# Storing x1's first channel with a graph's inputs, and later queue places for the gates' weights, spectra, loads and sixth product

## The chip, the core and the metric

The kernel runs on one core of one Trainium2 chip. The core has a matmul engine (TensorE, with its weight loads shown apart), a vector engine (VectorE, DVE in profiles), an activation engine (ScalarE, ACT), a general engine (GpSimd, POOL), a sync engine (SyncE, SP) that here only issues DMAs, and 16 DMA engines that all queues share. Each engine works through its own queue in order; a semaphore wait at the head of a queue holds everything behind it. The metric is the time of one execution on the device in microseconds (us).

## What is computed

64 graphs of N = 256 nodes with D = 256 features go through two layers. `adj` is each graph's matrix.

```python
# layer 0
norm_adj = deg**-0.5 * adj * deg**-0.5            # deg = row sums
x1 = layernorm(x + ((norm_adj + alpha*I) @ x) @ W.T + b)
# layer 1: three branches of x1
h      = relu(bn1(conv1(x1)))                     # a 1x1 convolution
x_conv = relu(bn2(conv2(h)) + x1)                 # 17 taps along the nodes
s      = x1 @ w_se.T + b_se
A      = exp(-dist(s))                            # squared distances of all pairs
x_nmp  = A @ relu(x1 @ w_msg.T + b_msg)
# a GRU cell joins them
gi = concat(x_conv, x_nmp) @ w_ih.T + b_ih
gh = x1 @ w_hh.T + b_hh
out = layernorm(x1 + gru(gi, gh, x1))
```

All numbers are 32-bit floats.

## The kernel before, in words

**Stages.** The graphs form four quarters of Q = 16. For each graph `layer0` (L383) makes x1, normalises it and stores it to DRAM as `x1_d` (L461, ACT's queue). `layer1` (L474) transposes x1 into `xn` (L464), multiplies by the conv1 weights (L487) and the message weights (L508), transforms h along the nodes into spectra in the big tile `VM`, and makes x_nmp. `graphs` (L1083) weaves layer 1 of one graph with layer 0 of the graph two further on.

When a quarter's 16 graphs are in `VM`, conv2 is done there as products of spectra (`products`, L611) with the transformed conv2 weights, which stream in from DRAM through six `u` buffers (`load_u`, L579, SP's queue), and then the inverse transform on VectorE, whose results go to DRAM as `xc_d` (L782).

Last come the gates of the quarter's graphs, `gru` (L914). Its product of 256x768 inputs with the weights is done by seven smaller products of halves (p1 to p7), which need four sums of halves of the inputs (`input_sums`, L893, POOL) and combined weights in `wall`. Each of the seven is three matmul calls, line L930.

**What overlaps.** Quarter 0's first 16 graphs run alone with the setup: in 13 parts (`weights`, L316) the conv2 weights are loaded (`load_taps`), multiplied on TensorE, summed on VectorE and POOL (L339, L340) and written to DRAM as `ud` by POOL's DMAs (L342). Then the gates' weights are prepared (`gate_weights`, L1156): a first piece loads them (L1160 to L1174), a second mends them on VectorE, further pieces subtract them from one another (L1189). The list `others` (L1193) says which of these pieces goes with which graph. Later, a quarter's first four gates (`EARLY`) run between the next quarter's last graphs, and the other twelve between its spectral products and inverse transform. The last quarter's 16 gates end the kernel, from about 1797 us on.

**The inputs of the gates.** `xn` has four blocks of 128 channels by 256 nodes: x1's first half with its first channel replaced by the constant 1 (so that the biases ride on that row, L471), two blocks of x_nmp, and x1's second half. It is stored whole as `xn_d` (L568) and read back into the tile `inputs` by `load_gate` (L838). Two more blocks of `inputs` receive the convolution, plus x1, through ReLU. For 28 of the graphs (`in_blocks`, L820: the first four of each quarter, and all of the last) `transposed` (L864) does this with VectorE's block transpose, and then POOL adds the x1 blocks (L875). That adds 1 in place of channel 0, so `load_gate` also loads channel 0 of x1 into a row of its own (L844), POOL adds it (L876), and the ReLU's bias is `less_one`, the bias less 1 in that row. The other 36 graphs add x1 in a DMA and transpose on TensorE.

**What sets the order.** The program is traced piece by piece; a scheduler at build time then gives each engine its order. It prefers what was traced earlier, but fills an engine that would be idle with later work that it believes ready. `tc.issue_after(i)` holds an instruction back: it keeps whatever is traced inside it, on i's engine, behind i in that engine's queue; it adds no wait. DMAs that SP and ACT issue share eight semaphores in turn, so such a DMA can also wait for an earlier one, of any kind, that used the same semaphore.

Of the kernel before, what the change touches and what calls it, by code (L numbers as in the profile page):

```python
# [9 lines left out]
F32 = mybir.dt.float32  # L10
AF = mybir.ActivationFunctionType
ALU = mybir.AluOpType
AX = mybir.AxisListType

P = 128
# [5 lines left out]
def bcast_rows(v, n, rows=P):  # L21

    return bass.AP(tensor=v.tensor, offset=v.offset, ap=[[0, rows], [1, n]])
# [3 lines left out]
def kernel(  # L27
# [38 lines left out]
    RB = 32  # L66
# [40 lines left out]

    def load_x(g):
        xin[g] = loads.tile([P, NCH, D], F32, name="x_t")
        nc.sync.dma_start(xin[g], x[g].rearrange("(c p) f -> p c f", p=P))  # L110

    def load(g):
        if g < B:
# [55 lines left out]
    bn_t = const.tile([P, D], F32)  # L169

    bn2_bias = const.tile([P, DCH], F32)
    less_one = const.tile([P, DCH], F32)

    def batch_norms(pool):

# [197 lines left out]
    xn_d = [dram.tile([P, 2 * DCH, N], F32, name=f"xn_d{g}") for g in range(B)]  # L373
    XN = {}
    ALONE = set()
    EXP, WEIGHED, NORMED = {}, {}, []
    gate = None
    EAGER = {0, Q - 4, Q - 3, Q - 2, *range(Q, Q + 13), 2 * Q + 5, 2 * Q + 6, 3 * Q + 5, 3 * Q + 6}
# [95 lines left out]
    def layer1(g, place):  # L474
# [9 lines left out]
        for c in range(NCH):  # L484
            p = bank("p_conv1")[:, : D + NSE]
            for k in range(DCH):
                nc.tensor.matmul(  # L487
                    p, x1T[:, k, c * P : (c + 1) * P], wc1[:, k, :], start=k == 0, stop=k == DCH - 1
                )
            nc.scalar.activation(  # L490
                h[:, c].rearrange("p (k a) -> p k a", k=DCH), p[:, :D].rearrange("p (a k) -> p k a", k=DCH), AF.Relu
            )
            EVICTED[g] = nc.scalar.copy(cols[:, c, :, :NSE], p[:, D:].unsqueeze(1).to_broadcast([P, 4, NSE])).ins
# [71 lines left out]
                    start=mc == 0, stop=mc == NCH - 1,  # L565
                )
        AGGREGATED[g] = nc.scalar.copy(xn[:, 1 : 1 + DCH], p).ins
        nc.scalar.dma_start(xn_d[g], xn)  # L568
        yield


# [4 lines left out]

    TILES, AWAY = [V], []

    def load_u(n, i):  # L579
        u = ustream.tile([P, DCH, D], F32, name="u")  # L580
        nc.sync.dma_start(
            u, ud[i][n * GC : (n + 1) * GC].rearrange("c g o -> (c g) o")[:D].rearrange("(p k) o -> p k o", k=DCH)
        )
        return u

    def product(p, j, v, u, onto=False):
# [225 lines left out]
            yield from output(q, n + 12, im + 3, re + 3)  # L812


    GATE, CONV, SUMS, OWN, CHANNEL = {}, {}, {}, {}, {}


    EARLY = 4

    def in_blocks(g):  # L820
        return g % Q < EARLY or g >= B - Q

    def load_conv(g):
        y = xc_d[g // Q][g % Q]
        if in_blocks(g):


            CONV[g] = gate.tile([P, DCH, N // RB, RB], F32, name="xc_blocks", tag="xc_g")
            for b in range(NB):
                nc.sync.dma_start(  # L830
                    CONV[g][b * RB : (b + 1) * RB],
                    y.rearrange("(s r) (k b j) -> b r k s j", r=RB, k=DCH, j=RB)[b],
                )
            return
        CONV[g] = gate.tile([P, NCH, D], F32, name="xc_g")
        nc.sync.dma_start(CONV[g], y.rearrange("(c p) d -> p c d", p=P))

    def load_gate(g):  # L838
        inputs = GATE[g] = gate.tile([P, 3 * DCH, N], F32, name="inputs")
        nc.sync.dma_start(inputs[:, : 2 * DCH], xn_d[g])  # L840
        if in_blocks(g):
            CHANNEL[g] = gate.tile([1, N], F32, name="channel", bufs=1)
            with nc.allow_non_contiguous_dma("one channel"):
                nc.sync.dma_start(CHANNEL[g], x1_d[g // Q][g % Q][:, 0:1].rearrange("n d -> d n"))  # L844

    def load_x1(g):
        OWN[g] = gate.tile([P, NCH, D], F32, name="x1_g")
        nc.sync.dma_start(OWN[g], x1_d[g // Q][g % Q].rearrange("(c p) d -> p c d", p=P))

    def sent(g):  # L850

# [12 lines left out]
    def transposed(g):  # L864

        inputs = GATE[g]
        xcT = inputs[:, 2 * DCH :]
        if in_blocks(g):
            to = xcT.rearrange("p k (s r) -> p k s r", r=RB)
            if g < B - Q:  # L870
                with tc.issue_after(WEIGHED[max(WEIGHED)]):
                    nc.vector.transpose(to, CONV.pop(g))
            else:
                behind(nc.vector.transpose(to, CONV.pop(g)))
            nc.gpsimd.tensor_tensor(xcT, xcT, inputs[:, 0 : 2 * DCH : 2 * DCH - 1], op=ALU.add)  # L875
            JOINED.append(nc.gpsimd.tensor_tensor(xcT[0:1, 0], xcT[0:1, 0], CHANNEL.pop(g), op=ALU.add).ins)  # L876
            with tc.issue_after(EXP[max(EXP)]):
                for k in range(DCH):
                    nc.scalar.activation(xcT[:, k], xcT[:, k], AF.Relu, bias=less_one[:, k : k + 1])
            return  # L880
        xc = CONV.pop(g)
        p = bank("p_xcT").rearrange("p (k n) -> p k n", k=DCH)
        for k in range(DCH):
            for c in range(NCH):
                nc.tensor.transpose(p[:, k, c * P : (c + 1) * P], xc[:, c, k * P : (k + 1) * P], ident)
        for k in range(DCH):
            nc.scalar.activation(xcT[:, k], p[:, k], AF.Relu, bias=bn2_bias[:, k : k + 1])
# [26 lines left out]
    def gru(g):  # L914
# [10 lines left out]
        def product(a, b, p=None):  # L925
            first = p is None
            if first:
                p = accbank("p_g")
            for k in range(HALF):
                nc.tensor.matmul(  # L930
                    p[:, : 3 * HD] if k == 0 else p[:, HD:], a[:, k], wall[:, b, k].rearrange("p t d -> p (t d)"),
                    start=first and k == 0, stop=True, skip_group_check=not first or k > 0,
                )
            return p
# [8 lines left out]
        yield  # L943
        if following:
            sent(g + 1)
        p6 = product(S[2], T2)
        mark(nc.vector.tensor_add(quarter(0, 1), first, p6), 1)  # L947
        nc.vector.tensor_add(quarter(1, 1), quarter(0, 1), p7)  # L948
        product(A12, B21, p1)
# [84 lines left out]
    def chain(*stages):  # L1034
        for stage in stages:
            yield from stage

    def take(stage, n):

        for _ in range(n):  # L1040
            if next(stage, "end") == "end":
                return
            yield

    def later(stage):
        yield
        yield from stage
# [74 lines left out]
    with tc.tile_pool(name="setup", bufs=1) as setup:  # L1122
# [31 lines left out]
        nc.gpsimd.tensor_copy(wmsg[0:1, 0], biases[:, NSE:])  # L1154

        def gate_weights():  # L1156
            for b, i, h in ((B11, 0, 0), (T1, 0, 1), (B21, 1, 0), (B22, 1, 1)):
                at = slice(h * HD, (h + 1) * HD)
                own = w_hhT[i * P : (i + 1) * P].rearrange("p (t d) -> p t d", t=3)
                nc.sync.dma_start(wall[:, b, 0, 0:1], own[:, 2:3, at])  # L1160
                nc.sync.dma_start(wall[:, b, 0, 1:3], own[:, 0:2, at])
                for k in range(DCH):
                    row = (D if i == 0 else 0) + k * P
                    nc.sync.dma_start(
                        wall[:, b, 1 + k], w_ihT[row : row + P].rearrange("p (t d) -> p t d", t=3)[:, :, at]
                    )
            nc.gpsimd.tensor_copy(less_one, bn2_bias)
            nc.gpsimd.tensor_tensor(less_one[:, 0:1], less_one[:, 0:1], unit, op=ALU.subtract)
            top = setup.tile([P, 3, 2, HD], F32, name="hh_top", tag="taps", bufs=2)
            nc.sync.dma_start(top.rearrange("p t h d -> p (t h d)"), bcast_rows(w_hhT, 3 * D))  # L1170
            rows = setup.tile([1, 2, 3, 2, HD], F32, name="gate_bias", tag="taps", bufs=2)
            for i, v in enumerate((b_hh, b_ih)):
                nc.sync.dma_start(rows[:, i].rearrange("p t h d -> p (t h d)"), v.rearrange("(a d) -> a d", a=1))
            nc.sync.dma_start(bn_t, bcast_rows(b_ih[2 * D :], D))  # L1174
            yield

            for b, i, h in ((B11, 0, 0), (T1, 0, 1), (B21, 1, 0), (B22, 1, 1)):
                with tc.issue_after(marks[-1][0]):
                    w = wall[:, b, 0]
                    nc.vector.tensor_sub(w[:, GR : GZ + 1], w[:, GR : GZ + 1], top[:, 0:2, h])  # L1180
                    nc.vector.tensor_sub(w[:, GN], w[:, GN], top[:, 2, h])
                    if i == 0:
                        nc.vector.tensor_add(w[0:1, GR : GZ + 1], rows[:, 0, 0:2, h], rows[:, 1, 0:2, h])
                        nc.vector.tensor_copy(w[0:1, GN], rows[:, 0, 2, h])
            yield

            for to, a, b in ((T3, B22, T1), (T1, T1, B11), (T2, B22, T1), (T4, B21, T2)):
                with tc.issue_after(marks[-1][0]):
                    nc.vector.tensor_sub(wall[:, to], wall[:, a], wall[:, b])  # L1189
                yield  # L1190
# [1 line left out]
        more_weights = gate_weights()  # L1192
        others = [weights(setup, i, scale2) for i in range(NPARTS)]  # L1193
        others[0] = later(others[0])
        others += [take(more_weights, i) for i in (1, 3, 2)]
        run(graphs(0, range(Q), others))
    ustream = ctx.enter_context(tc.tile_pool(name="ustream", bufs=6))

# [156 lines left out]
```

## Time and profile before

| | us |
|---|---|
| three runs | 2043.63, 2042.55, 2040.06 |
| median | 2042.55 |
| profiled execution | 2048.04 |
| its span, first to last instruction | 2046.3 |
| TensorE busy | 1984.9 |
| VectorE busy | 1396.4 |
| ScalarE busy | 964.7 |
| POOL busy | 698.1 |

The profile comes from one execution with the profiler on, and its lines name the engine, the source line, the operation, what is written and read, the shape, and the count. In a timeline line, the first number is the start, the second the time taken, both in us from the span's start; a bracket tells how long the engine had been idle and what ended that. In the table of waits the numbers are the total, the count and the longest. A window line has the stretch, its length, the busy time of TensorE, its weight loads, VectorE, ScalarE and POOL with instruction counts, the granted TensorE clock (1.00 is full), the busy share of the DMA engines and the GB/s they moved. In the chain, a line has start, length and name of one step in a sequence in which each step was released by the one before it. A line "x28: a/b/c" has the shortest, median and longest duration in ns. A busy TensorE is modelled from pipelined matmuls.

### The profile page before, as it was taken

How to read it: one execution, taken by the hardware profiler on the slowest of the kernel's cores; microseconds unless marked ns; L12 is line 12 of the kernel's file. 1: busy time of each engine (PE TensorE's matmuls, PEld its weight loads, DVE VectorE, ACT ScalarE, POOL GpSimd, SP SyncE). 2: the span in 40 equal slices, each digit the busy share in tenths (PEclk: the TensorE clock that was granted, in tenths of full speed). 3: DMA queues.
4: the chain of work that ended last, by engine and by line, in shares of the span. 5: the costliest groups of instructions: out<-in, count | busy, mean ns of one | idle time of the engine just before them, and what ended most of it. 6: DMA issues, size and time to landing. Idle time of an engine off the chain costs nothing. (4 is left out here: it accounts for less than half of the span.)

```text
span 2046.3 us, 26391 instructions
## 1 busy us (share of the span) xinstructions
PE 1984.9 (97%) x8157; PEld 1437.7 (70%) x8157; DVE 1396.4 (68%) x3199; ACT 964.7 (47%) x2285; POOL 698.1 (34%) x679
## 2 busy tenths in 40 slices
PE   7999999999999999999999999999999999999997
PEld 6878788878667766777777766777777855555554
DVE  6334447787567788764546888874445899877787
ACT  5666654567442234566653233556664233333333
POOL 4444411232532143223322234322331045445543
PEclk8999999999999999999999999999999999999999
DMA  4766557544555654343336665334344745443431
GB/s 133 221 202 207 182 193 240 169 140 135 138 149 192 212 126 134 115 129 109 103 109 185 211 170 134 119 117 125 97 116 142 259 124 135 127 100 87 102 87 54
DMA packets 269021, 298.05 MB, mean 146 GB/s; under 512 B 84276, under 2 KB 211336, under 8 KB 268882
## 3 DMA queue, kind: packets, MB, share of 16 engines
q1 hardware_dynamic: 208842, 200.37, 33.8%
q10 hardware_dynamic: 44472, 67.39, 9.3%
q0 software_dynamic: 15568, 28.62, 6.3%
q8 instruction: 66, 1.08, 0.2%
q14 instruction: 73, 0.60, 0.1%
HBM read 193.19 MB, written 103.06 MB: 145 GB/s over the span
## 5 line engine op out<-in xcount | busy, mean ns | idle before, releaser
L930 PE MATMUL p_g<-wall,sums 128*128 128x384 f32 x1536 | 534.0, 488 | 6.1 <-POOL sums L901 3.2
L930 PEld LDWEIGHTS p_g<-wall,sums 128*128 128x128 f32 x1536 | 284.8, 190 | 193.4 <-issue 9.6
L930 PE MATMUL p_g<-wall,inputs 128*128 128x384 f32 x1152 | 406.8, 489 | 12.2 <-DVE G L948 12.2
L930 PEld LDWEIGHTS p_g<-wall,inputs 128*128 128x128 f32 x1152 | 215.3, 190 | 167.2 <-DVE G L948 27.8
L356 POOL TENSOR_TENSOR ln_rs<-ln_rs,neg_half 128x2 f32<-128x2 f32 x129 | 95.2, 738 | 546.7 <-DVE ln_rs L355 411.0
L901 POOL TENSOR_TENSOR sums<-inputs 128x384 f32<-128x384 f32 x128 | 143.1, 1118 | 329.0 <-PE p_g L930 303.2
L554 DVE TENSOR_TENSOR aT<-aT,adjT 128x512 f32<-128x512 f32 x64 | 45.2, 706 | 200.5 <-ACT aT L551 200.4
L435 POOL TENSOR_TENSOR x_t<-x_t,b_t 128x512 f32<-128x512 f32 x64 | 101.9, 1592 | 215.3 <-ACT x L432 138.8
L589 PE MATMUL p_k<-u,VM 128*128 128x256 f32 x736 | 169.6, 380 | 2.8 <-DMA u<-ud 1.6
L589 PEld LDWEIGHTS p_k<-u,VM 128*128 128x128 f32 x736 | 138.5, 190 | 25.6 <-PE p_k L589 2.5
L364 ACT ACTIVATE x_g<-x_g,ln_mr,ln_rs 128x256 f32<-128x256 f32 x128 | 70.0, 593 | 169.4 <-DVE ln_mr L360 164.6
L977 ACT ACTIVATE G<-G 128x512 f32<-128x512 f32 (+1 forms) x129 | 81.0, 628 | 128.7 <-DVE G L1004 91.9
L440 PE MATMUL p_hT<-adjT,x 128*128 128x256 f32 x512 | 125.7, 389 | 5.8 <-ACT x L432 2.3
L487 PE MATMUL p_conv<-wc,xn 128*128 128x259 f32 x512 | 126.5, 389 | 4.2 <-ACT xn L471 3.5
L563 PE MATMUL p_nmp<-aT,msg 128*128 128x256 f32 x512 | 121.4, 380 | 2.2 <-DVE aT L554 2.2
L450 PE MATMUL p_out<-w,hT 128*128 128x256 f32 x512 | 121.5, 380 | 0.9 <-ACT hT L445 0.7
L901 POOL TENSOR_TENSOR sums<-inputs,sums 128x384 f32<-128x384 f32 x64 | 74.8, 1169 | 138.0 <-PE p_g L930 137.9
L508 PE MATMUL p_msg<-wmsg,xn 128*128 128x256 f32 x512 | 121.9, 381 | 0.0
L487 PEld LDWEIGHTS p_conv<-wc,xn 128*128 128x128 f32 x512 | 99.1, 194 | 27.1 <-ACT xn L471 4.3
L526 PE MATMUL p_dft<-fwd,h 128*128 128x240 f32 x512 | 114.1, 366 | 0.0
L950 ACT COPY G<-p_g 128x512 f32<-128x512 f32 x64 | 37.4, 584 | 155.9 <-PE p_g L930 107.2
L450 PEld LDWEIGHTS p_out<-w,hT 128*128 128x128 f32 x512 | 95.6, 190 | 21.2 <-ACT hT L445 2.9
(173 smaller groups left out, 3596.9 us busy)
## 6 DMA issues: line engine op xcount, KB each, us to landing
u<-ud SPq DMA_DIRECT2D x284, 256.0 KB
xn_d<-xn ACTq DMA_DIRECT2D x64, 512.0 KB
inputs<-xn_d SPq DMA_DIRECT2D x64, 512.0 KB
ud<-u_set POOLq DMA_DIRECT2D x39, 480.0 KB, 6.3
adj_t<-in_adj_dram SPq DMA_DIRECT2D x64, 256.0 KB
x_t<-in_x_dram SPq DMA_DIRECT2D x64, 256.0 KB
x_d<-x ACTq DMA_DIRECT2D x64, 256.0 KB
xc_d<-VM SPq DMA_DIRECT2D x64, 256.0 KB
```

Of the source, the lines that this page charges most:

```text
L356: nc.gpsimd.tensor_tensor(rs[:, : len(chunks)], rs[:, : len(chunks)], neg_half[:, : len(chunks)], op=ALU.pow)
L435: nc.gpsimd.tensor_tensor(x_t, x_t, b0_t.unsqueeze(1).to_broadcast([P, NCH, D]), op=ALU.add)
L440: nc.tensor.matmul(p[:, k, :], x1[:, mc, k * P : (k + 1) * P], adjT[:, mc, 1 - mc : 3 - mc, :].rearrange("p n q -> p (n q)"), start=mc == ...
L450: nc.tensor.matmul(p[:, c, :], hT[:, k, c * P : (c + 1) * P], w0[:, k, :], start=k == 0, stop=k == DCH - 1)
L487: nc.tensor.matmul(p, x1T[:, k, c * P : (c + 1) * P], wc1[:, k, :], start=k == 0, stop=k == DCH - 1)
L508: nc.tensor.matmul(p[:, c, :], x1T[:, k, c * P : (c + 1) * P], wmsg[:, k, :], start=k == 0, stop=k == DCH - 1)
L526: nc.tensor.matmul(p[:, t0 * FL : t1 * FL], h[:, c, k * P : (k + 1) * P], fwd[:, first : first + t1 - t0, :].rearrange("p t f -> p (t f)") ...
L563: nc.tensor.matmul(p[:, k, :], msg[:, mc, k * P : (k + 1) * P], aT[:, mc].rearrange("p n q -> p (n q)"), start=mc == 0, stop=mc == NCH - 1,)
L589: nc.tensor.matmul(p[:, j * D : (j + 1) * D], v[:, k, :], u[:, k, :], start=k == 0 and j == 0 and not onto, stop=k == DCH - 1, skip_group_ ...
L901: nc.gpsimd.tensor_tensor(S[i], x, y, op=op)
L930: nc.tensor.matmul(p[:, : 3 * HD] if k == 0 else p[:, HD:], a[:, k], wall[:, b, k].rearrange("p t d -> p (t d)"), start=first and k == 0, ...
L977: nc.scalar.activation(rz, rz, AF.Tanh, scale=0.5)
```

## The change

1. For the 28 graphs `in_blocks`, the store of `xn` is split: blocks 1 to 3 by ACT as before, block 0 without its first row by SP, and its first row is copied from channel 0 of `x1_d` by SP. After POOL has added the x1 blocks, a memset puts the constant 1 back into that row of `inputs`. The load of the channel, its addition and `less_one` are gone.
2. `load_conv`, `load_gate` and `load_x1` are held, in SP's queue, behind the last u load that was traced before them (`behind_u`).
3. In the early gates, the sixth product is held behind the last conv1 matmul that was traced before it.
4. The first piece of `gate_weights` is held, in SP's queue, behind the last x load traced before it (graph 16's).
5. The third piece of the last `weights` part (the sum and the stores of the spectra) is traced late in graph 13 in place of the end of graph 12, and the loads of the gates' weights at the end of graph 13 in place of its beginning.

```diff
     def load_x(g):
         xin[g] = loads.tile([P, NCH, D], F32, name="x_t")
-        nc.sync.dma_start(xin[g], x[g].rearrange("(c p) f -> p c f", p=P))
+        xin["last"] = nc.sync.dma_start(xin[g], x[g].rearrange("(c p) f -> p c f", p=P)).ins
...
+    CONV1 = {}
+    EARLY = 4
+
+    def in_blocks(g):
+        return g % Q < EARLY or g >= B - Q
...
-                nc.tensor.matmul(
+                CONV1[g] = nc.tensor.matmul(
                     p, x1T[:, k, c * P : (c + 1) * P], wc1[:, k, :], start=k == 0, stop=k == DCH - 1
-                )
+                ).ins
...
-        nc.scalar.dma_start(xn_d[g], xn)
+        if in_blocks(g):
+            nc.scalar.dma_start(xn_d[g][:, 1:], xn[:, 1:])
+            nc.sync.dma_start(xn_d[g][1:, 0], xn[1:, 0])
+            with nc.allow_non_contiguous_dma("one channel"):
+                nc.sync.dma_start(xn_d[g][0:1, 0], x1_d[g // Q][g % Q][:, 0:1].rearrange("n d -> d n"))
+        else:
+            nc.scalar.dma_start(xn_d[g], xn)
...
+    LAST_U = {}
+
+    def behind_u():
+        return tc.issue_after(LAST_U[0])
+
     def load_u(n, i):
         u = ustream.tile([P, DCH, D], F32, name="u")
-        nc.sync.dma_start(
+        LAST_U[0] = nc.sync.dma_start(
...
     def load_gate(g):
         inputs = GATE[g] = gate.tile([P, 3 * DCH, N], F32, name="inputs")
-        nc.sync.dma_start(inputs[:, : 2 * DCH], xn_d[g])
-        if in_blocks(g):
-            CHANNEL[g] = gate.tile([1, N], F32, name="channel", bufs=1)
-            with nc.allow_non_contiguous_dma("one channel"):
-                nc.sync.dma_start(CHANNEL[g], x1_d[g // Q][g % Q][:, 0:1].rearrange("n d -> d n"))
+        with behind_u():
+            nc.sync.dma_start(inputs[:, : 2 * DCH], xn_d[g])
...
             nc.gpsimd.tensor_tensor(xcT, xcT, inputs[:, 0 : 2 * DCH : 2 * DCH - 1], op=ALU.add)
-            JOINED.append(nc.gpsimd.tensor_tensor(xcT[0:1, 0], xcT[0:1, 0], CHANNEL.pop(g), op=ALU.add).ins)
+            JOINED.append(nc.gpsimd.memset(inputs[0:1, 0], 1.0).ins)
             with tc.issue_after(EXP[max(EXP)]):
                 for k in range(DCH):
-                    nc.scalar.activation(xcT[:, k], xcT[:, k], AF.Relu, bias=less_one[:, k : k + 1])
+                    nc.scalar.activation(xcT[:, k], xcT[:, k], AF.Relu, bias=bn2_bias[:, k : k + 1])
...
-        p6 = product(S[2], T2)
+        with tc.issue_after(CONV1[max(CONV1)]) if in_blocks(g) and g < B - Q else ExitStack():
+            p6 = product(S[2], T2)
...
         def gate_weights():
+            behind_x = ExitStack()
+            behind_x.enter_context(tc.issue_after(xin["last"]))
...
-            nc.gpsimd.tensor_copy(less_one, bn2_bias)
-            nc.gpsimd.tensor_tensor(less_one[:, 0:1], less_one[:, 0:1], unit, op=ALU.subtract)
...
             nc.sync.dma_start(bn_t, bcast_rows(b_ih[2 * D :], D))
+            behind_x.close()
             yield
...
-        others += [take(more_weights, i) for i in (1, 3, 2)]
+        last = others.pop()
+        others += [take(last, 2), chain(later(last), take(more_weights, 1)), take(more_weights, 3), take(more_weights, 2)]
```

More of the change, by code (lines that the diff above doesn't have):

```diff
@@ L171 @@
     bn2_bias = const.tile([P, DCH], F32)
-    less_one = const.tile([P, DCH], F32)
     def batch_norms(pool):
@@ L577 @@
     TILES, AWAY = [V], []
+    LAST_U = {}
+    def behind_u():
+        return tc.issue_after(LAST_U[0])
     def load_u(n, i):
         u = ustream.tile([P, DCH, D], F32, name="u")
-        nc.sync.dma_start(
+        LAST_U[0] = nc.sync.dma_start(
             u, ud[i][n * GC : (n + 1) * GC].rearrange("c g o -> (c g) o")[:D].rearrange("(p k) o -> p k o", k=DCH)
-        )
+        ).ins
         return u
@@ L812, in complex_end @@
             yield from output(q, n + 12, im + 3, re + 3)
[L815 to L821, printed above, removed]
+    GATE, CONV, SUMS, OWN = {}, {}, {}, {}
     def load_conv(g):
@@ L828, in load_conv @@
             CONV[g] = gate.tile([P, DCH, N // RB, RB], F32, name="xc_blocks", tag="xc_g")
[L829 to L833, printed above, removed]
+            with behind_u():
+                for b in range(NB):
+                    nc.sync.dma_start(
+                        CONV[g][b * RB : (b + 1) * RB],
+                        y.rearrange("(s r) (k b j) -> b r k s j", r=RB, k=DCH, j=RB)[b],
+                    )
             return
         CONV[g] = gate.tile([P, NCH, D], F32, name="xc_g")
-        nc.sync.dma_start(CONV[g], y.rearrange("(c p) d -> p c d", p=P))
+        with behind_u():
+            nc.sync.dma_start(CONV[g], y.rearrange("(c p) d -> p c d", p=P))
     def load_gate(g):
         inputs = GATE[g] = gate.tile([P, 3 * DCH, N], F32, name="inputs")
-        nc.sync.dma_start(inputs[:, : 2 * DCH], xn_d[g])
-        if in_blocks(g):
-            CHANNEL[g] = gate.tile([1, N], F32, name="channel", bufs=1)
-            with nc.allow_non_contiguous_dma("one channel"):
-                nc.sync.dma_start(CHANNEL[g], x1_d[g // Q][g % Q][:, 0:1].rearrange("n d -> d n"))
+        with behind_u():
+            nc.sync.dma_start(inputs[:, : 2 * DCH], xn_d[g])
     def load_x1(g):
         OWN[g] = gate.tile([P, NCH, D], F32, name="x1_g")
-        nc.sync.dma_start(OWN[g], x1_d[g // Q][g % Q].rearrange("(c p) d -> p c d", p=P))
+        with behind_u():
+            nc.sync.dma_start(OWN[g], x1_d[g // Q][g % Q].rearrange("(c p) d -> p c d", p=P))
     def sent(g):
```

## The prediction

> **What bounds the kernel.** I read the page first, then the waits of TensorE, then stretches of the timeline and the chain. The page and the table of waits say:
>
> ```profile
> PE 1984.9 (97%) x8157; PEld 1437.7 (70%) x8157; DVE 1396.4 (68%) x3199; ACT 964.7 (47%) x2285; POOL 698.1 (34%) x679
> q1 hardware_dynamic: 208842, 200.37, 33.8%
> PE p_g L930 <- DVE G L948: 12.2, 23, 1.5
> PE p_k L589 <- DMA u<-ud: 3.7, 6, 1.3
> PE p_conv L487 <- ACT xn L471: 3.5, 1, 3.5
> PE p_g L930 <- POOL sums L901: 3.2, 2, 1.6
> ```
>
> TensorE is the bound, and the change takes no matmul from it. So all that can be won is its idle time, 61.4 us, of which 11.7 lie in the first 30 us and 10.8 after its last matmul; some 39 are left. A wait of another engine counts only where TensorE then stands still. The costly places, from the timeline and from windows (PE busy second, granted clock third from the end):
>
> ```profile
> 112.32 0.42 ACT L393 ACTIVATE adjT<-adj_t 128x256 f32<-128x256 f32 x1 [4.93 <-DMA wall<-in_w_hhT_dram]
> 113.33 3.59 PE L487 MATMUL p_conv<-wc,xn 128*128 128x259 f32 x8 [3.52 <-ACT xn L471]
> 245.95 2.61 PE L440 MATMUL p_hT<-adjT,x 128*128 128x256 f32 x6 [1.67 <-DVE adjT L417]
> 107.00:120.00 13.00, 9.48 (x40) 7.69 (x39) 2.73 (x9) 6.30 (x18) 5.86 (x6) 0.87 0.64 186
> 236.00:252.00 16.00, 13.76 (x62) 10.52 (x61) 9.10 (x17) 8.67 (x24) 7.19 (x7) 0.89 0.54 174
> ```
>
> ACT stood still for 4.93 us until a gate weight's load had landed, which no operand of it needs; TensorE lost 3.52 us and then clock: 13 us x 0.13 = 1.7. At 246 it lost 0.57 + 1.67 and 16 x 0.11 = 1.8.
>
> **The clock rule.** The Trainium skill (TensorE: Matmul & The Clock Gate, section on HAM oscillation: no idle gaps of TensorE over about 3.4 us) would charge a clock loss at 113, with 3.52 us idle, but none at 246, where each gap is under 2 us. By the rule the 246 place is worth 2.2 us, by the window row 4.0. I take the row: short stalls close together cost clock too, and that counts against new stalls as well.
>
> **Gate weights' loads (L1160 to L1174).** They are traced with graph 13 but issued wherever SP was free: of 20, one at 34.8, sixteen between 65.6 and 107.5, and three (the broadcast row, two biases), which wait for their buffers, at 217.9 to 234.2. The edge holds all behind graph 16's x load, issued at 236.64. *Gain:* the 113 stall, 3.5 + 1.7 = **-5.2**. Bounds -5.2 to 0.
>
> *Price:* 16 weight loads now go in one row. Their issues took 1.87, 1.86 and 1.35 us (medians of L1160, L1161, L1164), 4 x 1.87 + 4 x 1.86 + 8 x 1.35 = 25.7 us: SP is busy from 237 to about 263. Queued behind are graph 17's adj load (issued at 239.6 before) and x load (253.4), then six u loads (257.3). Graph 17's adj is first read here:
>
> ```profile
> 267.51 0.42 ACT L393 ACTIVATE unused<-adj_t 128x256 f32<-128x256 f32 x1
> 268.58 0.60 PE L414 MATMUL p_adjT<-ident,adj_t 128*128 128x128 f32 x4
> ```
>
> Issued at 263 it has 4.5 us to land. In this crowded stage the x1 store issued at 66.1 was waited for until 75.2, 9.1 us; with the spectra's tap loads over by then it should be quicker (the store of 30.8 took 3.5). So it is 0 to 4.6 us late, ACT's degrees and TensorE's transpose behind it, plus 1.7 of clock; and the fix-ups of the weights on DVE (L1180, at 254 before) wait for the broadcast row, which now lands later. I take **+3**, bounds 0 to +10. The u loads are first needed at 279.9: hidden.
>
> **Last spectra sum.** Its DVE subtraction, POOL addition (2964 ns) and three POOL DMA issues (524 ns each) ran from 239.35 to 244.4. DVE's tiny L497 took 2.32 us beside the addition, and L417, 347 ns in the median, took 2.69 for two: the 246 stall, worth 4.0. The edit traces the sum some 10 us later. But it is held by the same two operations of graph 15 as before, and this scheduler issues early whatever is free:
>
> ```profile
> L1167 POOL COPY less_one<-bn_bias x1: 176/176/176, 16.3 to 16.3; 128x2 f32<-128x2 f32 x1
> ```
>
> This copy is traced with graph 13 too, and ran at 16.3 us. POOL had nothing else at 239.85. So the sum may well stay, only its DMAs falling behind L435. I take **-1**, bounds -4.0 to +2 (the u loads behind the later spectra stay hidden until 279.9).
>
> **The stored channel.** For 28 graphs (0 to 3, 16 to 19, 32 to 35, 48 to 63) the gates lose a load of 256 four-byte pieces on SP (L844, 0.54 us of issue) and a POOL addition (L876, 1046 ns); a one-row memset comes in. Nearest row: a POOL memset of 128x256, 332 ns. ReLU no longer waits for it. It counts in the last 220 us, where one loop through the buffers repeats every 14.02 us. From the chain:
>
> ```profile
> 1836.47 4.38 DMA inputs<-xn_d
> 1840.98 1.43 POOL inputs L875
> 1842.48 1.06 POOL inputs L876
> 1843.56 0.51 ACT inputs L879
> 1844.07 0.53 ACT G L993
> ...
> 1848.26 2.22 PE p_g L930 x6
> ```
>
> L876 drops out of this ring, but ACT then has two ReLUs and the copy of L941 in a row, so the ring shrinks by 0.2 to 0.8 us. TensorE is idle 221 - 215.96 = 5.0 us there (1797 to 2018), in bites of 0.2 to 0.7 a graph. I take **-3.5**, bounds -5.0 to 0.
>
> *Price:* each store turns from one ACT DMA into three: 384 KB on ACT, 127 rows of 1 KB on SP, and 256 four-byte pieces from DRAM to DRAM on SP, the last waiting in SP's queue until the x1 store has landed (adj, x and tap or u loads stand behind it meanwhile). **A rule that speaks against this:** by the Trainium skill (DMA: Bandwidth & Descriptors, section Why a DMA increments its semaphore by 16 and not by 1) a transfer is spread over the largest number of engines, at most 16, that divides its rows: 127 gives one. The page's q1 row makes 0.338 x 16 x 2046.3 / 208842 = 53 ns a packet. Spread over 16 that is 0.4 us; on one engine, 127 x 53 = 6.7 us, with later SP loads behind it on that engine. No transfer of this shape is in the trace. What covers it: the rows are ready at L471, 11 to 24 us before the xn buffer is written again (8.7 us from store to rewriting at the tightest, graph 19); loads of adj and x run a graph ahead; u loads lead by six products of 0.86 us. Only graphs 16 to 19 have their L471 (285 to 370) inside a stretch of u loads (281 to 379): 4 x about 1 us late. If the even spread held, 0; by the rule +4, less what the graph's own work covers. I take **+2**, bounds 0 to +14 (28 x 0.5, cover gone).
>
> **Gates' loads behind u.** With the edge, xc, inputs and x1 loads no longer stand ahead of u loads on SP: at 601.7 an x1_g load, itself waiting for an output to land, held six u loads. TensorE's waits for u are 3.7 us, 3.4 of them at 605, 642, 1094 and 1131. But at 1094 an x load (L110), waiting for DVE, was in front, and no edge touches it. I take **-2**, bounds -3.4 to +3 (a gate's load that comes late: the gates' own buffers are a graph ahead).
>
> **Sixth product behind conv1.** The two waits of 1.62 us for POOL (939, 1428) are this product's:
>
> ```profile
> 1428.13 2.20 PE L930 MATMUL p_g<-wall,sums 128*128 128x384 f32 x6 [1.62 <-POOL sums L901]
> ```
>
> Putting it later fills them with conv1. Against it: the memset sits in the first product's operand too, so the first and seventh products at the head of a quarter can no longer run before the transposed convolution is in. Without them TensorE lacks some work at 1417 to 1426. I take **-1.6** for both places, bounds -3.2 to +3.
>
> **Sum.** -5.2 + 3 - 1 - 3.5 + 2 - 2 - 1.6 = **-8.3 us**. The profiled execution took 2048.04 (span 2046.3, 1.7 around it) and would come to 2039.7. The runs' median, without the profiler, is 5.5 lower: 2042.55 - 8.3 = **2034**. Dropping the POOL copies for less_one is in time off the path: 0.
>
> **Rivals.**
> 1. *The stall moves with the gate weights.* Twenty loads together, where five once cost 5.2: two such stalls, 10.4 in place of +3, give -0.9: **2041.6**, no change. For it: the wait at 112 fell on a store that needed no weight. Against: the taps' loads have ended by 237.
> 2. *The edges bind nothing.* Sum, u loads and sixth product stay where the scheduler had them: -5.2 + 3 - 3.5 + 2 = -3.7: **2038.9**, no change either. The copy at 16.3 speaks for it; that the u waits have gate loads ahead of them, against.
> 3. *The single-engine row decides: slower.* Every other term as above makes -10.3. With a store exposing 0.51 us in each of 28 graphs (14.4 us) the kernel is 0.2% slower; at 0.85 it is +23.8, net +13.5: **2056**. For it: two more DMAs per graph, one of 6.7 us, on the queue that carries u. Against: 11 to 24 us of cover, and only four stores among u loads.
>
> **Chances.** My forecast 0.60, its own range 2027 to 2038; rivals 1 and 2 0.12 and 0.10; rival 3 and lesser losses 0.18. A difference under 0.2% (4.1 us) is what a measurement of this kernel can't tell from none. Faster 0.60, same 0.22, slower 0.18. Range for 8 in 10: 2026 to 2049.
>
> **What would show it.** Right: full clock and no idle TensorE at 100 to 120; weight loads after 237; TensorE's idle time after 1797 under 2 us; no wait for POOL sums near 939 and 1428. Wrong: ACT waiting for adj near 268, a dip of the clock at 240 to 275, waits of p_k for u at 285 to 380, waits of L471 for the stored xn.

## The result: 1.4% slower, and the profile after

The kernel with the change takes **2070.95 us** (median of four runs, 2063.55 to 2077.2), beside 2043.09 for the kernel before in as many runs. The ratio is 1.0138, with a 95% interval of 1.0101 to 1.0175. The forecast was 2034 us, in a range that ended at 2049: the kernel became slower where I had forecast a gain. The profiled execution took 2073.52 us (span 2071.7).

The page of the changed kernel first: busy times, and the queue of SP and ACT loads.

```profile
PE 1998.5 (96%) x8157; PEld 1449.4 (70%) x8157; DVE 1387.5 (67%) x3199; ACT 959.6 (46%) x2285; POOL 679.9 (33%) x677
q1 hardware_dynamic: 212426, 204.01, 34.9%
```

TensorE has the same 8157 matmuls and is busy for 13.6 us more. That is clock: outside the last 10 us it ran at half speed for 44.4 us of this execution, against 17.1 before, and of the difference, 27.3 us, half is lost. The rest of the 25.4 us of span is TensorE standing still, 11.8 us more. The waits of TensorE in the changed kernel (total, count, longest, in us):

```profile
PE p_k L605 <- DMA u<-ud: 9.8, 6, 3.9
PE p_g L940 <- DVE G L959: 9.6, 10, 1.5
PE p_hT L445 <- ACT x L437: 7.1, 12, 1.3
PE p_u L329 <- DVE taps L313: 5.7, 1, 5.7
PE p_dft L531 <- ACT scols L498: 3.0, 1, 3.0
```

The two waits for POOL sums are gone, as forecast, and so is the wait at 113. New are a stall for the taps of a setup load, a stall behind ACT (3.0 us), more of the short waits for ACT at L445 (2.3 us in 6 before), and u loads that come up to 3.9 us late. The table goes by stretch of the span: how long TensorE stood still (length less its busy time), and its mean granted clock. Two kernels of the experiments, e1 and a5, stand beside the pair for later. The stretches are the same times in each kernel, though in a slower one the later stages lie up to 26 us further on; measured back from the last product instead, the last row is 5.0, 0.4, 0.0 and 4.0, which reads the same.

| stretch, us | before | after | e1 | a5 |
|---|---|---|---|---|
| 30 to 95 | 0.0, 0.99 | 5.7, 0.92 | 1.5, 1.00 | 0.0, 0.99 |
| 95 to 130 | 3.5, 0.95 | 0.0, 1.00 | 0.0, 1.00 | 0.0, 1.00 |
| 235 to 280 | 3.6, 0.96 | 7.5, 0.92 | 9.5, 0.85 | 3.6, 1.00 |
| 280 to 400 | 2.0, 1.00 | 8.7, 0.94 | 1.9, 1.00 | 2.0, 1.00 |
| 400 to 1310 | 13.0, 1.00 | 16.1, 0.99 | 10.0, 0.99 | 8.7, 1.00 |
| 1310 to 1796 | 11.8, 1.00 | 13.7, 1.00 | 11.4, 1.00 | 12.1, 1.00 |
| 1796 to 2018 | 5.0, 1.00 | 0.0, 1.00 | 0.0, 1.00 | 3.8, 1.00 |

The last stage did what the forecast said. In the chain of the changed kernel, where the ring through `inputs`, POOL and ACT stood before, there is now one unbroken stretch of the gates' products:

```profile
1821.42 197.92 PE p_g L940 x606
```

The loss lies above all at 30 to 95 and 280 to 400. There are the windows of the two kernels, before and then after:

```profile
30.00:95.00 65.00, 65.00 (x320) 54.77 (x320) 27.85 (x73) 43.01 (x110) 25.54 (x25) 0.99 0.66 201
280.00:400.00 120.00, 118.01 (x573) 101.38 (x572) 80.53 (x192) 56.20 (x141) 18.91 (x15) 1.00 0.64 211
```

```profile
30.00:95.00 65.00, 59.33 (x275) 49.36 (x274) 22.73 (x59) 38.15 (x97) 23.18 (x22) 0.92 0.60 159
280.00:400.00 120.00, 111.31 (x504) 93.08 (x503) 68.67 (x160) 47.50 (x115) 15.23 (x12) 0.94 0.67 186
```

In these two stretches eight of the 28 graphs (0 to 3 and 16 to 19) store their `xn`, while the taps of the setup and the first u loads are on the way. In the timeline of the changed kernel (start, time taken, engine; a bracket is the idle time before and what ended it):

```profile
342.08 0.47 SPq L577 DMA_DIRECT2D xn_d<-x_d  x1
342.65 12.75 SPq L597 DMA_DIRECT2D u<-ud  x7
349.16 1.13 PE L605 MATMUL p_k<-u,ab 128*128 128x256 f32 x4 [1.36 <-DMA u<-ud]
352.98 3.35 PE L605 MATMUL p_k<-u,VM 128*128 128x256 f32 x7 [2.69 <-DMA u<-ud]
```

The channel's copy (L577) goes out, seven u loads follow it, and TensorE waits for u twice. The windows of the same kernel, 8 us before and 8 us after the copies at 342.1 and 378.7:

```profile
334.50:342.50 8.00, 8.00 (x40) 7.03 (x40) 4.66 (x11) 4.91 (x12) 1.03 (x1) 1.00 0.74 242
342.60:350.60 8.00, 6.33 (x30) 5.00 (x28) 7.93 (x14) 2.45 (x6) 1.87 (x1) 1.00 1.06 85
...
371.00:379.00 8.00, 8.00 (x40) 7.03 (x40) 7.43 (x24) 4.73 (x14) 1.38 (x2) 1.00 0.80 282
379.20:387.20 8.00, 8.00 (x41) 7.11 (x40) 7.96 (x17) 3.54 (x8) 4.14 (x1) 1.00 0.91 114
```

Read the last two columns, the DMA share and the GB/s, together. (The share adds up the recorded times of packets, so it can pass 1.) Ahead of a copy the DMA engines are busy for 0.74 and 0.80 of the time and move 242 and 282 GB/s. Behind it they are busy for 1.06 and 0.91, and move 85 and 114. They are held by something that moves hardly any bytes; below this is called the jam. A high DMA share alone would have looked like load.

### The profile page after: what moved, and what is told of

It is laid out like the page before. It is cut to its first block, busy times and chain, and to the rows that moved or that the text cites. A ratio compares the mean times of both kernels' runs of the same rounds, so it can differ in the third digit from the quotient of the medians.

```text
span 2071.7 us, 26436 instructions
## 1 busy us (share of the span) xinstructions
PE 1998.5 (96%) x8157; PEld 1449.4 (70%) x8157; DVE 1387.5 (67%) x3199; ACT 959.6 (46%) x2285; POOL 679.9 (33%) x677
## 3 DMA queue, kind: packets, MB, share of 16 engines
q1 hardware_dynamic: 212426, 204.01, 34.9%
## 5 line engine op out<-in xcount | busy, mean ns | idle before, releaser
L605 PE MATMUL p_k<-u,VM 128*128 128x256 f32 x736 | 174.2, 388 | 5.1 <-DMA u<-ud 3.7
L445 PE MATMUL p_hT<-adjT,x 128*128 128x256 f32 x512 | 127.7, 394 | 8.8 <-ACT x L437 7.1
L445 PEld LDWEIGHTS p_hT<-adjT,x 128*128 128x128 f32 x512 | 94.5, 196 | 26.3 <-ACT x L437 12.3
```

The costliest lines, as they stand in the source:

```text
L445: nc.tensor.matmul(p[:, k, :], x1[:, mc, k * P : (k + 1) * P], adjT[:, mc, 1 - mc : 3 - mc, :].rearrange("p n q -> p (n q)"), start=mc == ...
L605: nc.tensor.matmul(p[:, j * D : (j + 1) * D], v[:, k, :], u[:, k, :], start=k == 0 and j == 0 and not onto, stop=k == DCH - 1, skip_group_ ...
```

## The experiments

Times of a run are compared with runs of the kernel before beside it (2040.5 to 2041.3 us in these). Three theories stood at first. **R**: the 127-row store runs on one DMA engine, and loads behind it wait. **W**: the channel's copy waits at the head of SP's queue for the x1 store; the page of waits of SP shows that wait:

```profile
SPq L577 <- DMA x_d<-x: 83.5, 23, 8.9
```

**G**: the gate weights' loads, now in one row, are what stalls.

### Which part: the store, undone and alone

`a1_whole_store` stores `xn` whole and loads the channel with the gates as before; parts 2 to 5 stay.

```diff
-            nc.scalar.dma_start(xn_d[g][:, 1:], xn[:, 1:])
-            nc.sync.dma_start(xn_d[g][1:, 0], xn[1:, 0])
-            nc.sync.dma_start(xn_d[g][0:1, 0], <channel 0 of x1_d>)
+        nc.scalar.dma_start(xn_d[g], xn)
...
```

> The changed kernel with its first part undone: the inputs are stored whole by ACT again, and the gates load and add the channel as before. Parts 2 to 5 stay. Three theories of the 28 us: R, the 127-row store runs on one DMA engine and holds the loads issued behind it; W, the channel's copy waits in SP's queue for the x1 store; G, the gate weights' loads in one row stall ACT. By R or W the stalls at 81 and at 311 to 353 go (10.8 and 14.7 us with their clock) and the 4.6 us won in the last stage are lost again: about 2050 us. By G alone little changes: about 2070 us.

Measured: 2043.6, ratio 1.0012 (1.0005 to 1.0019). `a2_store_alone` is the opposite, part 1 on the kernel before.

> The kernel before with the first part alone (the split store, the memset, no channel load). By R or W the stalls at 81 and 311 to 353 are there, the last stage wins 4.6 us: about 2043 + 25 - 5 = 2063 us. By G it is only the last stage's gain: about 2038 us.

Measured: 2073.34, ratio 1.0165 (1.013 to 1.0199). So part 1 alone makes the whole loss; whether it makes more, the intervals don't tell. G falls as an account of it.

`a4_weights_early` undoes parts 4 and 5.

> The changed kernel with parts 4 and 5 undone: gate weights' loads and the last spectra sum placed as before. By G the 10.8 us at 247 to 273 fall to 4.5 and nothing else moves: about 2065 us. By R the weight loads share the crowded first 110 us with the single-engine stores, so what is won at 260 is lost there: 2070 us or more.

Measured: 2072.75, ratio 1.0159 (1.0135 to 1.0182): nothing comes back.

### The row of 127

`a3_row_spread` stores the 127 rows as 112 and 15 rows.

```diff
-            nc.sync.dma_start(xn_d[g][1:, 0], xn[1:, 0])
+            nc.sync.dma_start(xn_d[g][16:, 0], xn[16:, 0])
+            nc.sync.dma_start(xn_d[g][1:16, 0], xn[1:16, 0])
```

> The changed kernel with the 127 rows stored as 112 and 15 rows, which 16 and 15 divide, so that many DMA engines share them; queue, waits and bytes as they were, one DMA more. By R the late u loads at 311 to 353 and the late tap loads at 81 go: about 2050 us. By W, in which the copy of the channel holds SP, it stays near 2070 us.

Measured: 2063.52, ratio 1.0103 (1.0075 to 1.0131), some 7 us less than the changed kernel (1.0138 - 1.0103 = 0.0035), but the two intervals overlap, so that this is not shown to be a gain. R alone does not explain the loss, so the copy was taken on by itself.

### The copy: moved, and taken out

`b1_copy_on_act` issues the copy from ACT, where nothing waits for the x1 store any more.

```diff
-            with nc.allow_non_contiguous_dma("one channel"):
-                nc.sync.dma_start(xn_d[g][0:1, 0], <channel 0 of x1_d>)
+            with nc.allow_non_contiguous_dma("one channel"), tc.issue_after(AGGREGATED[g]):
+                nc.scalar.dma_start(xn_d[g][0:1, 0], <channel 0 of x1_d>)
```

> The changed kernel with the channel's copy issued from ACT's queue, behind the eviction of x_nmp, where the x1 store has long landed; the 127-row store stays on SP. W (the copy at the head of SP's queue waits for the x1 store, 84 us in 23 waits, and holds the loads behind it): those waits go, and with the row store's part left (the spread row gave back 7 to 10 us) the time is about 2050. R (the row on one DMA engine is all): what the spread row gave back is all there is to get, the copy's place gives nothing, 2068 to 2073. C (the copy's 256 pieces of four bytes load the DMA engines wherever they are issued): 2068 to 2073 too, but then the next run is faster than this one by 10 us or more.

Measured: 2075.3, ratio 1.0166 (1.0139 to 1.0193). W falls: with its wait gone from SP, nothing is gained.

`b3_no_copy` has no copy; the row is stored from `xn` in one piece of 1 KB.

```diff
-                nc.sync.dma_start(xn_d[g][0:1, 0], <channel 0 of x1_d>)
+            nc.scalar.dma_start(xn_d[g][0:1, 0], xn[0:1, 0])
...
```

> The changed kernel without the channel's copy: the row that it fills is stored from xn, with its constant, as one more row of 1 KB by ACT. What is left out: the residual of the convolution gets 1 in place of x1's first channel for 28 graphs. The 127-row store stays on SP. W: no SP wait for the x1 store, as in the run before it, so the same time within 3 us, about 2050. C: 10 us or more below the run before it. R: 2068 to 2073.

Measured: 2043.39, ratio 1.0014 (1.0007 to 1.0021), 32 us below the run before it. The copy is the loss wherever it is issued (C). The 127-row store is still there as it was, so R falls as the account of the loss. What the store costs by itself is small: b3 is as fast as a1, which has no such store. Its gain in the last stage (TensorE idle for 0.0 us at 1796 to 2018, in a1 3.5) is offset at 1310 to 1796 (13.3 for 11.0), so up to some 2 us there may be the store's.

The same place in b1, 8 us before and 8 us after the copy issued at 1411.3, shows the jam again, here with loads of the gates and of x behind it:

```profile
1403.00:1411.00 8.00, 8.00 (x38) 6.02 (x37) 3.83 (x6) 4.57 (x11) 1.27 (x1) 1.00 0.55 183
1413.00:1421.00 8.00, 4.19 (x22) 3.33 (x20) 3.39 (x19) 3.31 (x12) 2.04 (x3) 1.00 0.97 78
```

The DMA records of the trace tell more. The copy's 256 pieces are all recorded within half a microsecond after 1412.5, 7 or 9 ns each, and then no more of it is seen; but until about 1421 packets of other transfers take very long. Packets of 128 bytes on SP's queue, 13 ns in the ordinary case, took up to 4.6 us, those of 1 KB, ordinarily 46 ns, up to 6.2. Packets over 2 us in the whole trace: none in the kernel before and in a1, one in b3, 77 in the changed kernel, 98 in a2, 70 in a3, 77 in a4 and 220 in b1; in the changed kernel and in b1 every one of them starts within 9 us after a copy was issued. The Trainium skill (DMA: Bandwidth & Descriptors, section Back-pressure in remote DMA) says of writes to another core that stalled writes stall the engine's other queues as well. Here the target is this core's own DRAM. The trace fits the same picture: the copy was on ACT's queue, and packets of SP's queue stood. Whether they stood in the engines or at the memory, it doesn't show.

From the end of a DMA's issue to the last event on its semaphore, the medians over 28 are: the channel read in the kernel before 2.07 us; the copy in the changed kernel 7.55 (5.97 to 13.0).

### Reads or writes, and from where

The kernel before read the same 256 pieces 28 times without a loss, so `e1_copy_by_sbuf` reads them into a row on the chip, at the copy's place, and stores that row in one piece.

```diff
+            row = small.tile([1, N], F32, name="row", bufs=1)
             with nc.allow_non_contiguous_dma("one channel"):
-                nc.sync.dma_start(xn_d[g][0:1, 0], <channel 0 of x1_d>)
+                nc.sync.dma_start(row, <channel 0 of x1_d>)
+            with tc.issue_after(AGGREGATED[g]):
+                nc.scalar.dma_start(xn_d[g][0:1, 0], row)
```

> The changed kernel with the channel's copy in two steps: SP loads the 256 pieces of four bytes from x1's store into a row on the chip (where and when the copy was issued), and ACT stores that row as one piece of 1 KB behind the eviction of x_nmp. The 127-row store stays on SP. X (what jams the DMA engines is the 256 four-byte writes into DRAM; read as four-byte pieces the channel cost the kernel before nothing of the kind): 2043 to 2048, and no packet over 2 us. Y (four-byte pieces in the first layer, read or written, or SP's wait for the x1 store): 2065 to 2075.

Measured: 2042.66, ratio 1.0005 (0.9996 to 1.0015), no packet over 2 us. The same kind of place in e1, the 8 us behind the reads issued at 356.3 and 383.3:

```profile
356.70:364.70 8.00, 8.00 (x41) 7.05 (x40) 7.39 (x19) 3.40 (x7) 2.08 (x1) 1.00 0.86 286
383.80:391.80 8.00, 8.00 (x42) 7.07 (x41) 4.34 (x9) 5.69 (x15) 1.32 (x1) 1.00 0.76 236
```

Open was whether it takes small writes or a copy between two places in DRAM. `g1_small_writes` writes e1's row in two DMAs of 128 pieces of four bytes.

```diff
-                nc.scalar.dma_start(xn_d[g][0:1, 0], row)
+                for b in range(2):
+                    nc.scalar.dma_start(xn_d[g][0:1, 0, b::2], row[:, b::2])
```

> As the kernel that brings the channel over the chip in two steps (2042.7), but the row on the chip is written to DRAM by ACT in two DMAs of 128 pieces of four bytes, every other element each, in place of one piece of 1 KB. V (small writes into DRAM jam the DMA engines, wherever they come from): the loss is back, 2065 to 2075, with some 70 packets or more over 2 us. N (it takes a copy from DRAM to DRAM): 2042 to 2047, the price of 28 more DMAs on ACT at most, and hardly a packet over 2 us.

Measured: 2090.53, ratio 1.0233 (1.0208 to 1.0258), 96 packets over 2 us, each of which starts within 10.1 us after one of these writes. A DMA of 128 pieces took 6.2 us to land (median), the row in one piece in e1 1.35. The loss is back and larger. So it is **256 writes of four bytes into DRAM**, from DRAM or from the chip.

The size of this loss has a second cause in it. With one buffer for the row, SP's next read waits until the last row has been written, with u loads behind it:

```profile
SPq L578 <- DMA xn_d<-row: 122.2, 25, 7.5
```

In e1 this wait is 39.5 us in 12. How the loss divides between it and the jam is open, and the traffic behind two of the writes looked at fell less than in the changed kernel (200 to 211 GB/s at 334.2, 187 to 144 at 370.6). In b1, where SP waits neither for the x1 store nor for a row, the loss is there without such a wait. Not tried was whether the same small writes cost as much when they don't all go into one row of 1 KB.

### The other parts, without the copy

`d1_row_on_chip` gets the channel into `xn` with no DMA.

```diff
+            ROW[g] = small.tile([1, N], F32, name="row", bufs=1)
+            nc.vector.tensor_copy(ROW[g], p[0:1, 0])          # in x1_transposed
...
+            nc.gpsimd.tensor_copy(xn[0:1, 0], ROW.pop(g))      # behind the message products
...
+        nc.scalar.dma_start(xn_d[g], xn)
```

> The changed kernel with the same result got without a DMA: VectorE copies x1's first channel (1x256) from PSUM into a small tile, POOL puts it into xn after the message matmuls have read the constant, and ACT stores xn whole. The gates' side keeps the memset and loses load and addition. R and W alike (the loss is in the DMAs of the split store): the kernel with the whole store took 2043.6 with the old gates' side; the last stage's idle time of TensorE (3.5 us there, 0 in the changed kernel) goes: 2040, from 2038 to 2043. M (the memset in the first product's operand costs in the middle stages what it gains in the last): 2044 to 2050.

Measured: 2048.11, ratio 1.0033 (1.0022 to 1.0043), the upper case. VectorE and POOL got 28 operations more in layer 1, and TensorE waits 2.02 us for VectorE at 841 and at 1332 (L549), where e1's three waits on that line make 2.4 us together, 1.0 at the longest. The on-chip way is no gift. `d2_row_no45` is d1 without parts 4 and 5:

> As the run before it, with the last spectra sum and the gate weights' loads at their old places too (parts 4 and 5 undone). G (in the kernel with the whole store the gate weights' move gives 5.2 us at 113 and takes some 11 at 240 to 275): about 6 us under the run before it, 2034. If the move is worth what I forecast for parts 4 and 5 (-5.2 + 3 - 1 = -3.2): 3 us over it, 2043.

Measured: 2039.27, ratio 0.999 (0.9981 to 1.0). And `d4_row_no4` is d1 without part 4 alone:

```diff
-            behind_x.enter_context(tc.issue_after(xin["last"]))
```

> The kernel with the row put in on the chip, with part 4 alone undone: the last spectra sum and the gate weights' loads are traced late, but the loads are not held behind graph 16's x load. H (the hold is what puts twenty loads together at 237): the loads go out early again, 2039. T (tracing them late is enough to do so): 2048.

Measured: 2038.9, ratio 0.9987 (0.9978 to 0.9996). So part 4, the hold of the gate weights' loads, costs 1.0033 - 0.9987 = 0.0046, **9 us**, and part 5 nothing. The windows of d1 and then of d4:

```profile
235.00:280.00 45.00, 37.16 (x150) 28.23 (x149) 18.81 (x54) 21.38 (x58) 9.88 (x11) 0.81 0.65 199
```

```profile
235.00:280.00 45.00, 41.57 (x205) 33.56 (x204) 27.43 (x71) 25.89 (x72) 12.14 (x13) 1.00 0.56 188
```

4.4 us more of idle TensorE, and 0.19 of 45 us in clock (8.6): 13 us. The profiled execution of d1 stood 5 us over the median of its runs, so the 9 us of the medians is the better size. What happens there is in the timeline of the changed kernel:

```profile
261.31 0.34 ACTq L579 DMA_DIRECT2D xn_d<-xn  x1
261.70 0.42 ACT L398 ACTIVATE unused<-adj_t 128x256 f32<-128x256 f32 x1 [5.03 <-DMA wall<-in_w_ihT_dram]
262.59 0.77 PE L531 MATMUL p_dft<-fwd,h 128*128 128x240 f32 x1 [3.03 <-ACT scols L498]
```

This is a stall of the kind that stood at 112 before: a store of ACT waits until a gate weight's load, which used the same semaphore, has landed. It came with the loads to their new place, and there it is no accident of one execution: ACT's wait for such a load, 5.0 to 5.9 us, stands in the traces of a1, b3, d1 and e1 too.

`a5_loads_sixth` has parts 2 and 3 alone.

> Parts 2 and 3 alone on the kernel before: the gates' loads behind u, and the sixth product behind conv1. As forecast, -2 and -1.6: 3.6 us under the kernel before, 2037 to 2038. If parts 4 and 5 cost here the 8.8 us that they cost between the two kernels with the row put in on the chip: 2043.6 - 8.8 = 2035. If the two parts bind nothing that counts: 2041.

Measured: **2034.23**, ratio 0.996 (0.9945 to 0.9974). The two parts are worth 0.4%, twice what I gave them, and this kernel has, by coincidence, the time that I forecast for all five.

`f1_last_quarter` adds part 1 to a5 for the last quarter's 16 graphs, with e1's two-step store.

```diff
-        if in_blocks(g):
+        if g >= B - Q:
...
-            JOINED.append(nc.gpsimd.memset(inputs[0:1, 0], 1.0).ins)
+            if g >= B - Q:
+                JOINED.append(nc.gpsimd.memset(inputs[0:1, 0], 1.0).ins)
+            else:
+                JOINED.append(<the addition of the channel, as before>)
```

> Parts 2 and 3 on the kernel before, and for the last quarter's 16 graphs alone part 1 too, with the channel brought over the chip in two steps as before (256 pieces read into a row, the row stored as one piece). L (the channel's addition in the ring of the last stage is worth the 3.8 us that TensorE stands still there in the kernel with parts 2 and 3 alone, and the early gates of the other quarters don't profit): 2034.2 - 3.8 = 2030.5. E (what the last stage gains, the stores of the last quarter's layer 1 take back, as the whole set of 28 seems to do): 2033 to 2036.

Measured: 2032.61, ratio 0.9958 (0.9943 to 0.9973). Against a5 this is not told apart. In its profile TensorE is idle for 0.8 us at 1796 to 2018, where a5 has 3.8, but for 15.4 in place of 12.1 at 1310 to 1796, where the last quarter's layer 1 and spectra run. That speaks for E, in one execution. Both kernels are faster than the kernel before and the changed one.

## Why the prediction was wrong, step by step

**The step that failed: "The stored channel. Price", +2, bounds 0 to +14.** It priced the row of 127 and the place of the copy in SP's queue. It gave the copy's own 256 pieces nothing, and took away in the same breath "a load of 256 four-byte pieces", as if the one replaced the other. Read, they cost nothing that shows; written, they cost 1.0138 - 1.0005 = 0.0133, **27 us**. That is about 1 us for each of 28 copies, but not evenly: in the profiled execution most of it fell on the eight copies at 30 to 95 and 280 to 400. The prediction had named graphs 16 to 19 among the u loads, and the sign (waits of p_k for u at 285 to 380); what held the loads there it had not. The upper bound, half a microsecond for each store, was drawn from the wrong part of the store. The cover that I named for the row (u loads that lead by six products of 0.86 us) is 5.2 us, and the jam lasts some 8.

**The rule of one engine** fits, and was of little account. The 127-row store took 7.0 us at the least and 7.5 in the median in e1 from issue to landing, beside an estimate of 6.7; split into 112 and 15 rows, 2.3 and 2.1 in a3. By the rule the sum was +4; what b3 leaves room for is some 2. In the changed kernel, spreading the store gave back at most what the runs can't tell from nothing (0.0035), with about as many slow packets (70 for 77).

**Rival 3**, the slower one, came nearest in time (2056) with the row as its mechanism. Its sign was right, its cause was not, and I had kept the chance of all losses at 0.18 because no line of the profile made such a loss larger than the cover.

**Gate weights, gain -5.2.** The stall at 113 is gone in the changed kernel, but it is gone in a5 too, where the loads are as early as before. There the orders of work in the first 240 us are those of the kernel before; the load in question was issued at 96.9 in place of 99.6 and had landed at 104.0 in place of 111.9. In all six other traces with the loads at their early places (a2, a4, a5, d2, d4, f1) TensorE is never idle at 107 to 120. So the stall seems to have been one execution's. The prediction's own numbers fit that: the profiled execution stood 5.5 us over the median, and 2046.3 + 1.7 - 5.2 = 2042.8 is close to the median. I took the 5.5 off once as "the profiler" and then took the stall off again.

**Gate weights, price +3** was +9 (d1 against d4), inside its bounds. Rival 1 had this term right (two such stalls, 10.4 for +3), and its place was the one named (a dip of the clock at 240 to 275), though the wait is the semaphore's and not adj's.

**Last spectra sum, -1.** Nothing: d4 and d2 agree, and TensorE still waits 1.67 us for adjT at 240 in d4.

**The last stage, -3.5.** The size was right: 3.8 us of idle time in a5, none in e1. The memset took 301 ns beside the 332 of the row I chose:

```profile
L886 POOL MEMSET inputs<- x28: 301/301/303, 543.7 to 2037.8; 1x256 f32 x28
```

But e1 against a1 makes 1.0005 - 1.0012, 1.4 us, and f1 against a5 less than the runs can tell. Part of it is given back elsewhere, as f1's profile has it.

**u loads and sixth product, -2 and -1.6.** Right in kind, too small: together 0.4%, 8 us (5 to 11). In the traces 4.3 us of idle time went at 400 to 1310 and 1.3 in the last stage; the rest is not assigned. In the changed kernel these gains are under the jams: 16.1 us idle at 400 to 1310 in place of 8.7.

**The clock.** That stalls shorter than the 3.4 us of the rule in the prediction can cost clock too held: in the changed kernel two waits of 1.98 us, at 804 and 1296, each some 4 us behind a wait of 0.9, were followed by 3.4 us at half clock, while the single waits of 1.62 us at 939 and 1428 before cost none. Over this pair of executions 11.8 us of new idle time came with 13.6 us lost to half clock, about twice the idle time in all. The prediction counted the clock at the places of the gate weights and the last sum alone.

The terms as measured one by one, 0 for the stall at 113, +9 for the hold, 0 for the sum, -1 for the last stage, -8 for parts 2 and 3 and +27 for the copies, make +27 and fit the +28 measured. They don't add this way in each pair: on top of the copies, parts 4 and 5 cost nothing (a4).

## What to carry to other kernels

When the same pieces change direction, price them anew: here reading in pieces of four bytes was free where writing in them was not, and a row on the chip between the two made one piece of the write. Where the DMA share is high, look at GB/s beside it; engines that are busy and move little are a reason to look at the transfer just issued. And before a stall of one profiled execution is counted as a gain, ask whether the median of the runs has room for it.

## What the runs showed of the hardware

A DMA of 256 writes of four bytes into one 1 KB row of DRAM left the 16 DMA engines at a third to two fifths of their traffic for about 8 us (242 to 85 GB/s, 282 to 114), with packets of another queue held for up to 6.2 us. Its own packets are recorded at 7 or 9 ns each, so the table of queues, where q1 goes only from 33.8% to 34.9%, doesn't give it away. The same elements read from DRAM landed in 2.07 us and slowed nothing. The Trainium skill (DMA: Bandwidth & Descriptors, section Why small descriptors are slow) charges a small piece a few cycles and makes there no difference between reads and writes. By an estimate from that, 16 pieces on each of 16 engines would be far below the 7.55 us measured: the measurement decides.
